# Moving every SBUF tile by a few bytes: two unused tiles in a linear-attention kernel

## The chip, the cores and the metric

The kernel runs on one core of a Trainium2 chip. The metric is the device time of one execution in microseconds (us), as the median of several runs. Engines are called by the profile's names: PE (TensorE matmul), PEld (TensorE weight load), DVE (VectorE), ACT (ScalarE), POOL (GpSimd), SP (SyncE, which here issues nearly all the transfers).

## The reference

x has 4 batches of 512 tokens and 512 features. It is layer-normalised, goes through a gated linear attention of 16 heads of 128, and is multiplied by the SiLU of a router's mixture; the input is added at the end.

```python
def _lightning_attn(x, slope_rate, w_qkv, w_gate, w_out, norm_w):
    qkv = silu(einsum('bnf,of->bno', x, w_qkv))
    q, k, v = split(qkv.reshape(b, n, h, 3 * d), 3, axis=-1)
    def step(kv, blk):
        qi, ki, vi = blk
        o_inter = einsum('bhmd,bhde->bhme', qi * q_decay, kv)
        qk = einsum('bhmd,bhnd->bhmn', qi, ki) * diag_decay
        o_intra = einsum('bhmn,bhne->bhme', qk, vi)
        kv_new = block_decay * kv + einsum('bhmd,bhme->bhde', ki * k_decay, vi)
        return (kv_new, o_inter + o_intra)
    _, out = scan(step, kv0, (qb, kb, vb))
    out = norm_w * (out * rsqrt(mean(out * out) + EPS))
    gate = sigmoid(einsum('bnf,of->bno', x, w_gate))
    return einsum('bno,fo->bnf', gate * out, w_out)

xn = layernorm(x)
s = _lightning_attn(xn, ...)
scores = softmax(xn @ router_weight.T + router_bias)
topk_w, topk_idx = top_k(scores, 8)
ffn = xn * sum(topk_w) + einsum('tk,tkh->th', topk_w, expert_bias[topk_idx])
return x + s * silu(ffn)
```

## The kernel before

**Numbers.** The large products are made of fp32 operands split into a rounded high part and the rest (split_hi on ACT, split_lo on DVE or POOL), both kept as fp32r; three passes (high by high, high by low, low by high, PASSES) stand for one full product. The attention itself and the router's logits are plain fp32, which the trace shows as two matmuls each. Each large product is made of seven products of half-size blocks (PRODUCTS, a Strassen-Winograd scheme: B11, T2, T1, B21, T3, B22, T4 on the token side, A11, S2, S1, A12, S3, S4, A22 on the weight side).

**Stages.** First x is loaded, normalised, transposed by PE against ident and split into the blocks blk_B and blk_T; beside it the v units run (v_unit, lines 565 to 584, and the first two in plain form, d_v). Their moving operand is the weights, 512 columns in one run of 2048 bytes. Then come, for each pair of batches, 8 gate units and 16 q/k units (gate_unit, qk_unit), whose weights are stationary and whose moving operand is a block, `blocks[p, xn][:, :, xi, c]`: four runs of 128 columns, 512 bytes each. All of them go through unit(), whose matmul is line 506. Between the products of one unit the attention of the head before is run: scores_qk (sa line 662, transposes kt line 665), states (ss line 685), attend (o lines 747 and 749). The last stage is the output projection over 112 steps (p, m, g), each of 12 matmuls of 256 columns (acc, line 1218): the stationary operand is yr, the moving one wr. From step 54 on to 68, after every second step, ffn (line 811) adds two matmuls of 512 columns.

**Order.** The order on each engine is the order of the code (manual_schedule). Lists of functions, `after[j]`, are run behind the j-th product of a unit.

**Where tiles lie.** SBUF is taken from two sides. A pool made by left() or without a side grows upwards from the start, one made by right() downwards from the end, like two stacks. A pool's tiles lie one behind the other, each rounded up to 32 bytes per partition. From the left: const, wk, small, xa, then xb and later o and o2, and in the first stage vw and vout. From the right: stage, vraw, vsum; then hraw, hsum, hw, att, again, xc; at the end late. const comes first on the left, and holds small tiles of which several are not multiples of 128 bytes; it adds up to 3616 bytes. Nearly all large tiles are of 1024 bytes or multiples of 512, so a side's large tiles all begin at the same place modulo 128: 32 on the left, 96 on the right.

**Operands by side.** For the v units both operands are on the left (weights in vw, blocks in xa and xb). For q/k and gate units the weights are in hw, on the right; the blocks are on the left, except that for the second pair of batches B11, T2 and T1 are loaded into xc, on the right. The attention's tiles are all in att, on the right. In the output projection, wr of m = 0 lies in o and of m = 1 and 2 in xa (left), the others in late (right); yr of every second step lies in o2 (left), hw (right, parts 2, 3, 6, 7) or late (right, every third part after part 9); a part serves two steps. ident is a const tile.

```python
    def left(stack, name, bufs=1):
        return pool(stack, name, bufs, side="left", reuse_waits="tile")

    def right(stack, name, bufs=1):
        return pool(stack, name, bufs, side="right", reuse_waits="tile")
...
        tag, bufs = ("ws", None) if pool_ is hpools["w"] else ("yr", 2 if pool_ is op2 else 1)
...
                from_ = late if nsplit > 9 and nsplit % 3 == 1 else op2
```

reuse_waits="tile" makes a tile that takes over another's space wait for the release of just the tiles it overlaps.

Of the kernel before, what the change touches and what calls it, by code (L numbers as in the profile page):

```python
# [8 lines left out]
F32 = mybir.dt.float32  # L9
# [5 lines left out]
P = 128  # L15
# [35 lines left out]
def kernel(  # L51
# [26 lines left out]
    def pool(stack, name, bufs=1, **kw):  # L78
        return stack.enter_context(tc.tile_pool(name=name, bufs=bufs, **kw))
# [5 lines left out]
    def right(stack, name, bufs=1):  # L85
        return pool(stack, name, bufs, side="right", reuse_waits="tile")

    const = pool(ctx, "const")
# [14 lines left out]
        eng.tensor_tensor(lo, src, hi.bitcast(F32), ALU.subtract)  # L103


    slopes = const.tile([P, NH], F32, tag="slopes", name="slopes")
    rb = const.tile([P, E], F32, tag="rb", name="rb")
    rw = const.tile([P, FC, E], F32, tag="rw", name="rw")
# [1118 lines left out]
    for i, (p, m, g) in enumerate(steps):  # L1227
# [15 lines left out]
        if g == 0:  # L1243
            k, first = PRODUCTS[m][2:]
            if m < 3:
                q, tag = (ps_sc, "sc") if k == 2 else (ps_mm, "mm")
# [92 lines left out]
```

## Time and profile before

| | us |
|---|---|
| median of 3 runs | 1063.43 |
| lowest, highest | 1061.49, 1067.32 |
| span of the profiled execution | 1062.1 |

The page gives the span and no separate time of that execution; the median of the runs lies 1.3 us above it. The granted TensorE clock is 0.999 on average.

| matmuls, by shape | count | busy, mean ns of one |
|---|---|---|
| acc, 128x256 | 1344 | 281 |
| u_qk, 128x512 (four groups) | 1344 | 393 to 397 |
| u_g, 128x512 (four groups) | 672 | 392 to 401 |
| u_v, 128x512 (four groups) | 588 | 389 to 396 |
| d_v, 128x512 | 96 | 391 to 402 |
| o, 128x128 | 896 | 275 |
| sa, 128x128 | 512 | 275 |
| ss, 128x128 | 384 | 274 |
| kt, 128x128 transposes | 192 | 273 |

Matmuls are pipelined, so these busy times overlap. The chain of work that ended last, asked for over a stretch of time, is merged into pieces with a count; a piece of matmuls alone, divided by its count, gives the time from one matmul's start to the next one's.

### The profile page before, as it was taken

To read this page: it belongs to the slowest core of one execution; us is meant where nothing else is said; L and a number is where in the kernel's file an instruction comes from. 1 tells how busy PE (TensorE), PEld (TensorE's weight loads), DVE (VectorE), ACT (ScalarE), POOL (GpSimd) and SP (SyncE) were. 2 spreads that over 40 slices of the span, in tenths; PEclk is the share of its full clock that TensorE was granted. 3 is DMA by queue.
4 is the path that set the end of the run, shared out by engine and by line. 5 is a ranking of instruction groups with operands and counts; after the bars stand their busy time and mean duration, and the time that the engine had idled before them with its cause. 6 is when DMAs were issued, how large, how long until landed. Compare 5 with 4: busy or idle time off the path is not lost.

```text
span 1062.1 us, 17614 instructions
## 1 busy us (share of the span) xinstructions
PE 1043.7 (98%) x6338; PEld 923.6 (87%) x6338; DVE 636.5 (60%) x1017; ACT 558.5 (53%) x969; POOL 687.7 (65%) x698
## 2 busy tenths in 40 slices
PE   8999999999999999899999999999999999999997
PEld 7888888888888878788888888888888889999997
DVE  6665543356565777675554555455555557698667
ACT  5555554655555445454554655555555546574632
POOL 4887782757788677677778687878678753124013
PEclk9999999999999999999999999999999999999999
DMA  6456747523434365564664423443233336989863
GB/s 226 167 200 245 269 146 230 161 85 115 135 116 147 130 213 186 186 216 147 238 233 125 132 86 115 154 130 114 85 106 128 105 134 215 337 303 306 283 219 102
DMA packets 128838, 185.12 MB, mean 174 GB/s; under 512 B 11104, under 2 KB 72688, under 8 KB 127856
## 3 DMA queue, kind: packets, MB, share of 16 engines
q1 hardware_dynamic: 127856, 183.56, 52.2%
q8 instruction: 50, 0.82, 0.3%
q10 hardware_dynamic: 896, 0.44, 0.1%
q14 instruction: 36, 0.29, 0.1%
HBM read 115.26 MB, written 70.80 MB: 175 GB/s over the span
## 4 chain that ended last, share of the span: by engine, by line
PE 91%; DVE 5%; DMA 2%; issue 1%; ACT 0%; SPq 0%; POOL 0%; DVEq 0%; ACTq 0%; POOLq 0%
PE u_qk L506 27%; PE u_g L506 14%; PE acc L1218 13%; PE u_v L506 13%; PE sa L662 5%; PE o L747 5%; PE o L749 4%; PE ss L685 4%; PE kt L665 2%; PE d_v L536 2%; PE lg L322 1%; DMA raw_v<-in_w_v_dram 1%; DVE wosum L736 1%; DVE yS L710 1%; DMA x<-in_x_dram 1%
## 5 line engine op out<-in xcount | busy, mean ns | idle before, releaser
L1218 PE MATMUL acc<-wr,yr 128*128 128x256 f32 x1344 | 163.4, 281 | 1.3 <-DVE a_o L890 1.3
L1218 PEld LDWEIGHTS acc<-wr,yr 128*128 128x128 f32 x1344 | 161.5, 190 | 3.2 <-DVE a_o L890 1.7
L506 PE MATMUL u_qk<-blk_T,ws_qk 128*128 128x512 f32 x576 | 148.0, 397 | 0.0
L759 POOL TENSOR_TENSOR sqs<-sqs,sq 128x512 f32<-128x512 f32 x60 | 78.2, 1303 | 91.4 <-ACT sq L758 91.4
L506 PEld LDWEIGHTS u_qk<-blk_T,ws_qk 128*128 128x128 f32 x576 | 105.7, 188 | 21.4
L103 POOL TENSOR_TENSOR ws_qk<-sum_qk,ws_qk 128x512 fp32r<-128x512 f32 x64 | 88.8, 1395 | 40.8 <-ACT ws_qk L100 40.8
L506 PE MATMUL u_qk<-blk_B,wa_qk 128*128 128x512 f32 x384 | 100.1, 396 | 0.0
L870 POOL TENSOR_TENSOR u<-u,x 128x256 f32<-128x256 f32 x28 | 32.3, 1175 | 100.3 <-DVE u L869 69.7
L103 DVE TENSOR_TENSOR yr<-yin,yr 128x1024 fp32r<-128x1024 f32 x56 | 75.6, 1355 | 35.2 <-ACT yr L100 29.8
L747 PE MATMUL o<-at,vin 128*128 128x128 f32 x512 | 88.4, 275 | 0.0
L506 PEld LDWEIGHTS u_qk<-blk_B,wa_qk 128*128 128x128 f32 x384 | 70.9, 188 | 15.0
L100 ACT CAST yr<-yin 128x1024 fp32r<-128x1024 f32 x56 | 58.4, 1046 | 44.6 <-PE acc L1218 34.4
L550 ACT ACTIVATE k<-k 128x512 f32<-128x512 f32 x64 | 40.4, 632 | 74.3 <-DVE k L497 74.3
L751 DVE SCALAR_TENSOR_TENSOR y<-o,nw,gt 128x512 f32<-128x512 f32 x64 | 48.0, 751 | 51.3 <-PE o L749 51.3
L747 PEld LDWEIGHTS o<-at,vin 128*128 128x128 f32 x512 | 74.8, 191 | 2.5
L506 PE MATMUL u_g<-blk_T,ws_g 128*128 128x512 f32 x288 | 76.5, 401 | 0.0
L671 ACT ACTIVATE kd<-kt,kdecay 128x384 f32<-128x384 f32 x64 | 37.2, 581 | 73.9 <-PE kt L665 73.9
L758 ACT ACTIVATE sq<-o 128x512 f32<-128x512 f32 x60 | 35.9, 598 | 74.3 <-POOL sqs L759 43.2
L749 PE MATMUL o<-qd,st 128*128 128x128 f32 x384 | 74.2, 275 | 0.0
L103 POOL TENSOR_TENSOR ws_g<-sum_g,ws_g 128x512 fp32r<-128x512 f32 x32 | 41.4, 1295 | 48.6 <-ACT ws_g L100 48.6
L689 DVE SCALAR_TENSOR_TENSOR st<-st,bdecay,ss 128x128 f32<-128x128 f32 x128 | 41.7, 346 | 52.1 <-ACT st L687 49.9
L673 POOL TENSOR_TENSOR qd<-q,dec 128x384 f32<-128x384 f32 x64 | 70.9, 1129 | 0.0
(199 smaller groups left out, 2434.4 us busy)
## 6 DMA issues: line engine op xcount, KB each, us to landing
yin<-y SPq DMA_DIRECT2D x56, 512.0 KB, 4.5
v<-vo_v SPq DMA_DIRECT2D x64, 256.0 KB, 2.4
raw_qk<-in_w_head_dram SPq DMA_DIRECT2D x64, 256.0 KB, 4.1
vin<-v SPq DMA_DIRECT2D x64, 256.0 KB, 3.4
y<-yS SPq DMA_DIRECT2D x64, 256.0 KB, 2.1
y<-y SPq DMA_DIRECT2D x48, 256.0 KB, 2.2
woin<-wo SPq DMA_DIRECT2D x18, 512.0 KB, 5.7
x<-in_x_dram SPq DMA_DIRECT2D x32, 256.0 KB, 4.6
```

Of the source, the lines that this page charges most:

```text
L100: nc.scalar.copy(hi, src)
L103: eng.tensor_tensor(lo, src, hi.bitcast(F32), ALU.subtract)
L506: nc.tensor.matmul(ps, lhsT, rhs, start=(first and c == 0 and n == 0), stop=(c == KC - 1 and n == len(PASSES) - 1), skip_group_check=not f ...
L662: nc.tensor.matmul(pa[:, c], k[:, c], q[:, c], start=True, stop=True)
L673: nc.gpsimd.tensor_tensor(qd[s], q[:, 1:], d[:, 1, None, :].to_broadcast([P, NT - 1, P]), ALU.mult)
L685: nc.tensor.matmul(ps[:, c], kd[s][:, c], v_of(b, h, c), start=True, stop=True)
L689: nc.vector.scalar_tensor_tensor(r[:, c], r[:, c - 1], bdecay[:, h : h + 1], ps[:, c], ALU.mult, ALU.add)
L747: nc.tensor.matmul(o, v_of(b, h, c), at[s][:, c], start=True, stop=(c == 0))
L749: nc.tensor.matmul(o, st[s][:, c - 1], qd[s][:, c - 1], start=False, stop=True)
L751: nc.vector.scalar_tensor_tensor(y, po, nw[:, h : h + 1], gts[s], ALU.mult, ALU.mult)
L759: nc.gpsimd.tensor_tensor(sq[b], sq[b], s1, ALU.add)
L1218: nc.tensor.matmul(acc[t // 2][:, t % 2], yr[:, yi, bass.ts(t, P)], wos[m, g // NQ][:, wi, g % NQ], start=(first and g == 0 and n == 0 and ...
```

## The change

Two tiles are allocated and never used: one of 24 fp32 (96 bytes per partition) as the first tile of const, on the left, and one of 8 fp32 (32 bytes) in a pool of its own, the first on the right, which stays open to the end. All tiles that come after them on their side lie 96 bytes higher or 32 bytes lower. The large tiles on the left then begin at 0 modulo 128 in place of 32, those on the right at 64 in place of 96.

```diff
+    margin = right(ctx, "margin")
+    const.tile([P, 24], F32, tag="margin", name="margin_left")
+    margin.tile([P, 8], F32, tag="margin", name="margin_right")
     slopes = const.tile([P, NH], F32, tag="slopes", name="slopes")
```

## The prediction

> **What bounds the kernel now.** I read the page from the engines down: busy shares first, then the chain of work that ended last, then that chain piece by piece in short stretches.
>
> ```profile
> PE 1043.7 (98%) x6338; PEld 923.6 (87%) x6338; DVE 636.5 (60%) x1017; ACT 558.5 (53%) x969; POOL 687.7 (65%) x698
> PE 91%; DVE 5%; DMA 2%; issue 1%; ACT 0%; SPq 0%; POOL 0%; DVEq 0%; ACTq 0%; POOLq 0%
> ```
>
> TensorE (PE) is busy nearly throughout and carries 91% of the chain, so the end moves only if a matmul takes more or less time from its start to the next one's start. The busy durations in the costliest groups (281 ns for a 256-column matmul, 397 ns for a 512-column one) overlap and can't be added. The chain can: a piece "x24" is 24 matmuls with nothing between them, so its length over its count is the true price of one. First two long pieces of the whole chain (start us, us, what):
>
> ```profile
> 99.23 88.67 PE u_v L506 x390
> ...
> 682.17 12.41 PE u_qk L506 x54
> ```
>
> 88.67/390 = 227.4 ns for the v units, whose 512 moving columns lie in one run; 12.41/54 = 229.8 ns for the q/k units, whose 512 columns are four runs of 128. Next the same chain, asked for over 945 to 1003 us, where each piece between two ffn matmuls holds two steps of the output projection, and so tells apart where their operands lie:
>
> ```profile
> 944.98 26.45 PE acc L1218 x224
> ...
> 971.90 2.73 PE acc L1218 x24
> ...
> 978.40 2.87 PE acc L1218 x24
> ...
> 981.74 2.79 PE acc L1218 x24
> ```
>
> The ffn matmuls follow steps 54, 56, 58 and so on, so the first x24 piece is steps 55 and 56, the second 59 and 60, the third 61 and 62. By the code, step 55 streams wr from the right side against weights yr on the left, and step 56 the other way round (parts 27 and 28; part 28 comes from the pool late). Steps 59 and 60 have both operands on the left. Same work, same clock (1.00 in this stretch): 2.73/24 = 113.8 ns with the operands on opposite sides, 2.87/24 = 119.6 ns on the same side. So a matmul's price here depends on where its operands lie modulo 128, and one step between the two prices is 0.14/24 = 5.8 ns. The third piece, left/left and then left/right, lies between (116.3 ns). This is what the change can move.
>
> Last, the stretch of 198 to 240 us:
>
> ```profile
> 209.88 0.89 PE sa L662 x8
> 210.77 0.33 PE kt L665 x3
> ...
> 215.08 1.34 PE ss L685 x12
> 216.42 4.14 PE u_qk L506 x18
> ```
>
> kt is the one frequent matmul whose moving tile is not at 32 modulo 64: it streams ident. The const tiles, each rounded up to 32 bytes, add up to 3616 = 28 x 128 + 32 bytes, and the left side behind them is said to lie at 32, so const starts at 0; ident stands behind 1408 = 11 x 128 bytes, also at 0. It costs 0.33/3 = 110 ns. sa and ss, also of 128 columns but with both tiles on the right, cost 0.89/8 = 111.3 and 1.34/12 = 111.7. (kt is a transpose, so part of the difference may be its own.)
>
> **The change part by part.** It adds no instruction, wait or transfer: nothing writes or reads the two tiles, and the order on every engine and queue stays. What stands in the same place is not changed either: every left tile goes up by 96 bytes and every right tile down by 32, so a left and a right tile that take each other's space come 128 bytes closer. The nearest pair that must not touch, the end of o2 and the start of att and late, is 192 bytes apart by the tile sizes and will be 64. So no new wait arises; an overlap would have cost a wait of PE on a release, of up to the 6.5 us that PE's longest wait group has now.
>
> What is left is addresses. Left minus right stays 64 modulo 128. What changes is the place within a block of 64 bytes: every large tile lay half a block off (32 and 96), and now begins a block. Priced by groups of matmuls, counts from the groups by shape:
>
> A, output projection (acc): 1344 of 256 columns, now 26.45/224 = 118.1 ns in the chain's long piece.
> B, 512 columns in one run (u_v 588, d_v 96, pu and spare 32): 716, now 227.4 ns.
> C, 512 columns in four runs (u_qk 1344, u_g 672): 2016, now 229.8 ns.
> D, two-pass fp32 (o 896, sa 512, ss 384, lg 128): 1920, now about 111.5 ns.
>
> No row shows A to C with aligned tiles, so I bound them. Below: they cost what kt shows per 128 weights loaded, 110 ns for A, and twice that for 512 columns. A saves 8.1 x 1344 = 10.9 us, B 7.4 x 716 = 5.3, C 9.8 x 2016 = 19.8, D 1.5 x 1920 = 2.9: 38.9 us. Above: the pairs on opposite sides fall to the dearer state (the slower rival below, +11 us). I take one step, 5.8 ns, off each of A, B and C: (1344 + 716 + 2016) x 5.83 ns = 23.8 us. My reason is that the prices lie on steps of that size (113.8 and 119.6), that a run starting half a block off touches one block more than it has to; if PE fetches by such blocks, which no row shows and which I suppose, every one of these matmuls pays for one. The value lies between the ends, nearer the rows of acc themselves than kt, which is another kind of matmul. D I leave at 0.
>
> The const tiles go the other way: ident from 0 to 96. The 272 transposes that stream it (kt 192, pt 64, pw 16) at 1.5 ns dearer are 0.4 us. Other engines' tiles move too; DVE, ACT and POOL hold 5% of the chain together, and I cost them at nothing because PE covers them; with the cover gone a change of 1% in all of DVE's 636.5 us would be 6.4 us. Transfers likewise:
>
> ```profile
> v<-vo_v SPq DMA_DIRECT2D x64, 256.0 KB, 2.4
> y<-yS SPq DMA_DIRECT2D x64, 256.0 KB, 2.1
> ```
>
> One leaves the left side, one the right, 256 KB each, 0.3 us apart, and only 2% of the chain is DMA. The cover is thinnest here (us, busy us of PE, PEld, DVE, ACT and POOL, clock, DMA share, GB/s):
>
> ```profile
> 895.00:945.00 50.00, 49.41 (x402) 48.06 (x401) 38.90 (x53) 32.81 (x43) 10.96 (x9) 1.00 0.91 316
> ```
>
> At 0.91 of the DMA engines, acc can run some 9% faster before the loads of y and x set the pace; one step off 118.1 is 5%, so it passes. If it did not, A's 5% in those 50 us, 2.5 us, would be lost.
>
> Two rules of the Trainium skill pull apart on this. "TensorE: Matmul & The Clock Gate", section Back-to-back issue gap, gives a warm matmul N/2.4 + 2.5 ns, 109.2 at 256 columns and 215.8 at 512; if alignment restored all of that, A, B and C would give back an estimated 12.0 + 8.3 + 28.2 = 48.5 us. "SBUF — State Buffer", section Who interferes with whom, says that PE never waits on anyone, and its read ports for weights and moving data are independent; by that addresses cost nothing and the sum is 0. The 113.8 against 119.6 ns above contradicts the second in this kernel. The same page's section on operand start alignment says it is about legality and that nothing was timed.
>
> Sum: 1062.1 - 23.8 + 0.4 = 1038.7 us of span. The median of the runs, 1063.43, lies 1.3 us above the profiled span, so 1040.0.
>
> **The rivals.** Only the distance between operands matters. It is 64 modulo 128 before and after, so all prices stay: 1063.4 us. For it: the one address effect that the profile shows is one of sides. Against it: the opposite-side price is still above kt's. The same time follows if the tiles are laid out otherwise than described.
>
> Slower: with both streams starting on a block's edge, the weights' and the moving data's reads meet at every block, and pairs on opposite sides lose their advantage. Place: u_qk and u_g with blk on the left and weights on the right, all 1008 of the first pair of batches and, since three of seven blocks then lie in xc on the right, 576 of the second, 1584 x 5.83 = 9.2 us; in acc some 720 matmuls on opposite sides at 117 on average rise to 119.6, 1.9 us. With the 0.4 us of ident: 1063.4 + 11.5 = 1074.9. It decides from 5.3 us on, about 910 such matmuls. For it: same-side pairs do pay today. Against: nothing shows why 0 and 64 should meet where 32 and 96 don't.
>
> All of the excess over kt goes: 1063.4 - 38.9 + 0.4 = 1024.9; the forecast's own lower end.
>
> **How the numbers follow.** One step or more gained (forecast and its lower end): 0.57. Distance alone, or nothing done: 0.16. Meeting streams: 0.27. A measurement here tells about 0.5%, 5.3 us, from no change. So faster 0.57, same 0.16, slower 0.27; likeliest 1040, with its own range 1025 to 1056 (a third of a step). Leaving out a little below 1025 and the worse half of the slower case, the range is 1023 to 1075.
>
> **What would show it.** Right: u_v's long piece near 221 ns a matmul in place of 227.4, 18 of u_qk in about 4.03 us in place of 4.14, acc x24 pieces all below 2.73 to 2.79 us, kt at 0.33 to 0.34 for three. Wrong: the same pieces with the same lengths (the distance rival), or acc pieces of different sides at 2.87 and u_qk x18 above 4.2 (meeting streams). A DMA or DVE share of the chain that grows past 895 us would show a gain that was not passed on. What would overturn it all is a change in DVE, ACT or POOL durations large enough to reach PE.

## The result and the profile after

The changed kernel takes 1067.34 us (median of 22 runs, 1064.11 to 1073.41), the kernel before 1065.07 us (22 runs): ratio 1.0034, 95% interval 1.0022 to 1.0047. By the ratio that is 3.6 us slower, less than 0.5% (the two medians lie 2.3 us apart). The forecast was 1040, a gain; the measured time lies in the stated range of 1023 to 1075 only because that range also took in the rivals. The profiled execution after has a span of 1067.0 us against 1062.1.

Shares of the engines and of the chain of the page after (first line: busy us, share of the span, instructions):

```profile
PE 1049.5 (98%) x6338; PEld 924.4 (87%) x6338; DVE 637.5 (60%) x1017; ACT 558.4 (52%) x969; POOL 688.0 (64%) x698
PE 90%; DVE 4%; DMA 2%; issue 1%; POOL 1%; ACT 1%; SPq 1%; DVEq 0%; POOLq 0%; ACTq 0%
```

The same instructions, the same bound. What differs is again in the pieces of the chain (start us, us, what), here those of the whole chain of the changed kernel:

```profile
119.58 69.62 PE u_v L509 x306
...
199.00 12.60 PE u_qk L509 x54
...
218.18 4.20 PE u_qk L509 x18
...
688.48 12.45 PE u_qk L509 x54
...
950.55 26.63 PE acc L1221 x228
...
1000.75 57.01 PE acc L1221 x489
```

u_v: 69.62/306 = 227.5 ns, against 227.4 before. Both its operands lie on the left, and starting at 0 modulo 128 in place of 32 gave it nothing. u_qk of the first pair of batches: 12.60/54 = 233.3 and 4.20/18 = 233.3 ns, against 4.14/18 = 230.0: dearer. Of the second pair, three of whose seven blocks lie beside the weights on the right: 12.45/54 = 230.6 against 229.8. acc: 26.63/228 = 116.8 against 118.1: cheaper. Between the ffn matmuls of the output projection, and at the transposes, in two stretches of the same chain of the changed kernel:

```profile
977.64 2.79 PE acc L1221 x24
...
984.17 2.87 PE acc L1221 x24
```
```profile
212.49 0.33 PE kt L668 x3
```

The first piece is steps 55 and 56 (2.73 us before), the second steps 59 and 60 with both operands on the left: 2.87 us, to the digit as before. kt streams ident from 96 modulo 128 in place of 0, and its 0.33 us stay.

To see where the 4.9 us between the two spans are, I took from both traces the time from each matmul's start to the next one's, put it down to the earlier of the two, and told the operands' sides apart by their pools (ns is the mean of the differences under 250 ns, us their sum with all; for u_v and d_v only where the next matmul is of the same kind):

| moving, weights | count | before ns, us | after ns, us |
|---|---|---|---|
| u_qk, u_g: left, right | 1583 | 229.5, 379.7 | 233.2, 386.0 |
| u_qk, u_g: right, right | 432 | 230.3, 102.2 | 228.9, 101.7 |
| acc: right, left | 504 | 117.8, 60.0 | 115.1, 58.0 |
| acc: left, right | 216 | 116.1, 25.1 | 117.2, 25.3 |
| acc: left, left | 360 | 120.6, 43.4 | 120.7, 43.5 |
| acc: right, right | 263 | 119.6, 33.1 | 119.6, 33.1 |
| u_v, d_v: left, left | 668 | 227.3, 154.4 | 227.4, 156.7 |
| fp32, two-pass: right, right | 1791 | 108.6, 194.5 | 108.7, 194.7 |

One row carries the loss: u_qk and u_g with the block on the left and the weights on the right, 1583 x 3.7 ns = 5.9 us. acc with wr right and yr left gives back 504 x 2.7 = 1.4 us. acc with both operands on one side keeps its price; u_qk and u_g with both on the right get 1.4 ns cheaper, 0.6 us. By the ns alone the sum is +4.4 us, inside the interval of the ratio (2.3 to 5.0 us). The 2.3 us more of u_v and d_v are nearly all in two places where PE waited for DVE, some 0.9 us at 19.7 us (a wait for w_A_v) and 1.1 us at 118.2 us (for e_v); the mean price of a u_v matmul is the same. The profiled execution of e1 below has the second wait and not the first, that of e4 the first and not the second, so neither belongs to the change alone; what makes them was not looked for.

### The profile page after: what moved, and what is told of

It reads as the page before. It is cut to its first block, busy times and chain, and to the rows that moved or that the text cites. A ratio compares the mean times of both kernels' runs of the same rounds, so it can differ in the third digit from the quotient of the medians.

```text
span 1067.0 us, 17614 instructions
## 1 busy us (share of the span) xinstructions
PE 1049.5 (98%) x6338; PEld 924.4 (87%) x6338; DVE 637.5 (60%) x1017; ACT 558.4 (52%) x969; POOL 688.0 (64%) x698
## 4 chain that ended last, share of the span: by engine, by line
PE 90%; DVE 4%; DMA 2%; issue 1%; POOL 1%; ACT 1%; SPq 1%; DVEq 0%; POOLq 0%; ACTq 0%
PE u_qk L509 27%; PE acc L1221 14%; PE u_g L509 14%; PE u_v L509 12%; PE sa L665 5%; PE o L750 5%; PE o L752 4%; PE ss L688 4%; PE kt L668 2%; PE d_v L539 1%; PE lg L325 1%; DMA raw_v<-in_w_v_dram 1%; DVE wosum L739 1%; DVE yS L713 1%; POOL w_S_v L103 1%
```

## The experiments

Two theories were left. D: a matmul's price goes by the distance between its moving operand and its weights, with a period of 256 bytes or more. (A distance is given modulo 256; both theories are about where a tile starts in its partition.) Before the change the right side began 192 bytes behind the left modulo 256; the change moved the sides towards each other by 128 and made it 64, which modulo 128 is the same. P: the place within 64 or 128 bytes counts. The change altered both at once; the first two experiments alter one each.

**e1: the distance alone.** One unused tile of 128 bytes on the left; every tile keeps its place modulo 128, the distance is 64.

```diff
+    const.tile([P, 32], F32, tag="margin", name="margin_left")
     slopes = const.tile([P, NH], F32, tag="slopes", name="slopes")
```

> One unused tile of 128 bytes on the left alone. Every tile keeps its place modulo 128 (left 32, right 96), but the right side now begins 64 bytes behind the left modulo 256, as after the change, where it was 192. Theory D (only the distance between a matmul's two operands counts, modulo 256 or more): the time of the changed kernel, ratio to before 1.002 to 1.005; 18 matmuls of u_qk with blk left and weights right 4.20 us in place of 4.14; acc with wr right and yr left 114 ns in place of 118. Rival P (the place modulo 64 or 128 counts): as before, ratio 1.000 +- 0.001, 4.14 us.

Measured: ratio 1.0039 (1.0022 to 1.0056). The chain of e1 from 198 us on:

```profile
210.36 0.33 PE kt L666 x3
...
216.05 4.20 PE u_qk L507 x18
```

The price of the changed kernel without its alignment: u_qk and u_g left/right (the moving operand on the left, the weights on the right) 233.2 ns, acc right/left 115.3.

**e2: the place alone.** by_row goes from the left to the first place on the right, so that both sides sink by 32 bytes: 0 and 64 modulo 128 as after the change, and the distance of before.

```diff
-    by_row = const.tile([P, 2], F32, tag="rest_of", name="rest_of")
+    margin = right(ctx, "margin")
+    by_row = margin.tile([P, 2], F32, tag="rest_of", name="rest_of")
```

> No unused tile; the tile by_row (32 bytes with its rounding) moves from the left to the first place on the right. Both sides lie 32 bytes lower: left at 0 and right at 64 modulo 128 as after the change, their distance as before (192 modulo 256). Theory D: the time of before, ratio 1.000 +- 0.001, 18 u_qk matmuls 4.14 us, acc right/left 118 ns. Rival P: the time of the changed kernel, ratio 1.002 to 1.005, 4.20 us, 114 ns.

Measured: ratio 1.0000 (0.9984 to 1.0015), and in its chain

```profile
216.66 4.14 PE u_qk L507 x18
```

as before. The table's prices are those of before as well (229.6; acc 117.8 and 116.0). So the place within 64 or 128 bytes moves nothing that can be seen here, and the distance moves all that the change moved. P falls. The pairs whose two operands both lie on the left are a further control: in the twelve profiled kernels the left side stands at eight different places modulo 256, and u_v costs 227.3 to 227.7 ns in all of them, acc left/left 120.5 to 120.7 in all but v1, which alone moves yr against wr.

**e3 and e4: two more distances.** Unused tiles of 64 and 192 bytes on the left: distances 128 and 0. (Here and for s1 to s3 the comment behind a line names its run.)

```diff
+    const.tile([P, 16], F32, tag="margin", name="margin_left")    # e3
+    const.tile([P, 48], F32, tag="margin", name="margin_left")    # e4
```

> One unused tile of 64 bytes on the left: both sides at 96 modulo 128, the right 128 bytes behind the left modulo 256. Theory D with a period of 128: pairs on opposite sides now cost what pairs on one side cost: acc 120 ns throughout (some 720 matmuls by 3 ns, +2 us), u_qk and u_g between the 228 and 231 ns of their right/right matmuls, so +-3 us: ratio 0.999 to 1.005. With a period of 256: a price of its own for opposite pairs, not that of one side. Rival P: left tiles move by 64 within a block of 128, so pairs of one side on the left change from 120 and 227 ns too; under D these stay.

> One unused tile of 192 bytes on the left: both sides at 96 modulo 128, and at the same place modulo 256 (distance 0; one side against itself has distance 0 as well). Theory D: opposite pairs cost what one side costs, acc 120 ns throughout (+2 us), u_qk and u_g 228 to 231 ns: ratio 0.999 to 1.005. If e3 and e4 have the same prices the period is 128, else 256 or more. Rival P: as e3, since both sides lie at the same places modulo 128.

Measured: e3 1.0047 (1.0031 to 1.0063), e4 0.9989 (0.9975 to 1.0003). Chain of e3, at 198 to 240 us, and of e4 at the same place:

```profile
216.74 4.18 PE u_qk L507 x18
```
```profile
216.28 4.10 PE u_qk L507 x18
```

Both sides start at 96 modulo 128 in both kernels, and yet u_qk and u_g left/right cost 232.4 ns in one and 227.8 in the other: the period is not 128. At distance 0, acc costs 120.3 to 120.6 on opposite sides, as on one side (119.8 and 120.6); u_qk and u_g cost 227.8, below every price of theirs until then. I had expected 228 to 231 there.

**s1 to s4: the odd distances**, one run each for their prices. Unused tiles of 32, 96 and 160 bytes on the left, and for the fourth one tile less there:

```diff
+    const.tile([P, 8], F32, tag="margin", name="margin_left")     # s1
+    const.tile([P, 24], F32, tag="margin", name="margin_left")    # s2
+    const.tile([P, 40], F32, tag="margin", name="margin_left")    # s3
```
```diff
-    ones = const.tile([P, 1], F32, tag="ones", name="ones")
-    mhalf = const.tile([P, NT], F32, tag="mhalf", name="mhalf")
+    halves_ones = const.tile([P, NT + 1], F32, tag="mhalf", name="mhalf")
+    mhalf, ones = halves_ones[:, 0:NT], halves_ones[:, NT:]
```

> One unused tile of 32 bytes on the left: the right begins 160 bytes behind the left modulo 256. Measured so far, one u_qk or u_g matmul with blk left and weights right costs 229.6 ns at 192, 232.5 at 128, 233.2 at 64, 227.8 at 0. Theory D, smooth in the distance: between its neighbours, about 231 ns, acc on opposite sides 117 to 119.5; one side against itself stays at 120 (acc) and 227.4 (u_v). Rival (blocks of 64 bytes count, so that 32 is a straddle): a price outside the two neighbours.

> One unused tile of 96 bytes on the left and none on the right: left at 0 modulo 128 as in the change, right at 96 as before; distance 96. Theory D, smooth: 232.5 to 233.2 ns for u_qk and u_g, acc right/left between 115.4 and 119.4, left/right 117.3 to 119.4. Rival (blocks): outside these.

> One unused tile of 160 bytes on the left: distance 32. Theory D, smooth: u_qk and u_g between 227.8 and 233.2 ns, about 230.5; acc right/left 115.4 to 120.6, left/right 117.3 to 120.3. Rival (blocks): outside these.

> The const tiles mhalf and ones share one tile, which takes 32 bytes off the left: distance 224. Theory D, smooth: u_qk and u_g between 227.8 and 229.6 ns, acc right/left 117.8 to 120.6, left/right 116.4 to 120.3; u_v and acc on one side stay at 227.4 and 120. Rival (blocks): outside these.

The runs took 1072.4, 1071.8, 1068.9 and 1069.3 us beside one of 1063.4 of the kernel before; a single run each, so only their prices are used. D in its smooth form was wrong: u_qk and u_g lie outside their neighbours at 32, 96 and 160 and at the upper edge at 224, and acc lies outside at 96. The rival's forecast, a price outside, thus came true for u_qk and u_g, whose odd distances cost 233.2 to 234.0 ns, and for acc at 96, but not for acc at 32, 160 and 224. Why the prices run as they do over the distance is open. Put together, though, the eight distances give each price twice. With wr on the right and yr on the left, moving minus weights is the distance; with wr on the left it is 256 minus the distance, from another kernel:

| moving minus weights, modulo 256 | acc, wr right, ns | acc, wr left, ns | u_qk and u_g, left/right, ns |
|---|---|---|---|
| 0 | 120.6 (e4) | 120.3 (e4) | 227.8 (e4) |
| 32 | 117.5 (s3) | 117.6 (s4) | 233.3 (s4) |
| 64 | 115.1 (after), 115.3 (e1) | 116.1 (before) | 229.5 (before) |
| 96 | 120.1 (s2) | 120.4 (s1) | 233.4 (s1) |
| 128 | 119.5 (e3) | 119.4 (e3) | 232.4 (e3) |
| 160 | 117.8 (s1) | 118.6 (s2) | 234.0 (s2) |
| 192 | 117.8 (before) | 117.2 (after) | 233.2 (after, e1) |
| 224 | 118.8 (s4) | 119.0 (s3) | 233.2 (s3) |

The two columns of acc agree within 1.0 ns in every row, though one streams from the right and the other from the left and, but for 0 and 128, each row comes from different kernels. In this table side and place drop out; what is left is moving minus weights modulo 256. It also has a sign: 64 and 192 are not alike, clearly for u_qk and u_g (229.5 against 233.2). The change swapped just these two. A price of acc is a mean, though, over stretches at two levels, near 113 and near 118 ns, and both occur at 64 and at 192: at 64, 57% (before) and 71% (after) of the differences are 115 ns or less, at 192 only 15% and 34%.

**d0 and v1: the distance within one side, and a faster kernel.** By the table u_qk and u_g cost least at 0 and acc at 64. d0 takes 64 bytes off the left (distance 0, this time 256 modulo 512):

```diff
-    ones = const.tile([P, 1], F32, tag="ones", name="ones")
-    mhalf = const.tile([P, NT], F32, tag="mhalf", name="mhalf")
+    few = const.tile([P, NT + 3], F32, tag="mhalf", name="mhalf")
+    mhalf, ones = few[:, 0:NT], few[:, NT : NT + 1]
...
-    by_row = const.tile([P, 2], F32, tag="rest_of", name="rest_of")
+    by_row = few[:, NT + 1 :]
```

v1 adds two pads that put yr 64 bytes before wr:

```diff
                 op2 = left(o_stack, "o2", 2)
+                op2.tile([P, 48], F32, tag="pad", name="pad_left", bufs=1)
...
         if i == 16:
+            late.tile([P, 16], F32, tag="pad", name="pad_right", bufs=1)
             load_eb(late)
```

> mhalf, ones and by_row share one const tile, which takes 64 bytes off the left: distance 0 modulo 256 again, but 256 modulo 512, where e4 had 0 modulo 512. Theory D with a period of 256: the prices of e4, u_qk and u_g at 227.8 ns with blk left and weights right, acc 120 to 120.6 on opposite sides, ratio 0.998 to 1.000. With a period of 512 or more: other prices, 229 ns and more. Theory P has no account of e4's 227.8.

> As d0_left_minus_64, and two pads inside pools (192 bytes at the start of o2, 64 bytes behind yr in late) put yr 64 bytes before wr modulo 256 in 104 of the 112 steps, whichever side they lie on. Theory D: the price goes by the distance whatever the side, so acc on one side falls from 120.5 too; at 115.2 to 116.4 ns for some 1247 matmuls (the best prices of the runs so far) it saves 5 to 7 us against d0, ratio to before 0.990 to 0.994. Rival (what counts is being on two sides): acc pairs of one side stay at 120, ratio 0.997 or above.

Measured: d0 0.9988 (0.9978 to 0.9999), v1 0.9935 (0.9915 to 0.9954). The chain of d0, pieces of the output projection from its whole chain and from 930 to 1010 us:

```profile
942.24 27.34 PE acc L1218 x228
...
993.33 58.67 PE acc L1218 x489
```
```profile
970.04 2.86 PE acc L1218 x24
...
973.37 2.86 PE acc L1218 x24
...
976.69 2.86 PE acc L1218 x24
```

With all distances 0, every piece is 2.86 us, 119.2 ns a matmul, whatever the sides; x489 gives 120.0. v1, its chain from 935 us on and its whole chain:

```profile
976.24 2.83 PE acc L1219 x24
...
982.84 2.72 PE acc L1219 x24
...
986.02 2.83 PE acc L1219 x24
```
```profile
97.68 88.67 PE u_v L506 x390
...
989.32 57.60 PE acc L1219 x489
```

57.60/489 = 117.8, with left/left pairs down from 120.5 to 118.0 and right/right from 119.8 to 116.5 in the table's measure: a pair on one side gets cheaper when its operands move apart within that side. But the table's price for 64 did not carry over whole: at that distance acc costs 116.5 to 118.0 ns in v1, also with wr right and yr left (117.1, where the changed kernel has 115.1). So the distance is not all that sets the price of acc. u_v, untouched by the pads, is at 227.4. v1 beats both kernels, by 0.65% the one before and, by the two ratios, by about 1% the changed one. The gain of d0 is in u_qk and u_g (227.8 ns) less the loss in acc; v1 takes that loss back. Of the 5 to 7 us that I expected of the pads against d0, the means of acc (120.2 to 117.6 over 1343 matmuls) explain 3.6; the medians differ by 4.9; where the rest comes from was not looked for. v1's ratio met its forecast, then, though its price of acc did not. d0 and e4 have the same prices at 0 and at 256 modulo 512, which is what makes the period 256; it was tried at this one distance.

## Why the prediction was wrong

**What bounds the kernel**: right. But for the two short waits above, all that moved, moved in the chain's matmuls.

**No new wait, transfers and other engines at nothing**: right as far as the runs show. e2, which moves all large tiles by 32 bytes, has the ratio 1.0000, and e1, with the distance alone, the ratio of the change; the matmuls' prices, +4.4 us, leave nothing of the measured 3.6 us for other engines to explain.

**"Every large tile lay half a block off (32 and 96), and now begins a block", and one step of 5.8 ns off each of A, B and C**: this is the step that failed. B, u_v, went from 227.4 to 227.5 ns. A on one side stayed (2.87 us in 24); on opposite sides it fell by 2.7 ns one way round and rose by 1.1 the other. C rose by 3.7 ns in 1583 matmuls, those with the block on the left. The term put at -23.8 us measured some +4.2 (A -1.1, B 0, C +5.3). e2 shows that the place within a block is worth nothing by itself. The block was supposed, not read: the two prices of acc, 113.8 and 119.6 ns, told of the distance between operands, and I took the size of that effect as the price of another. The size was misread too: 113.8 ns is one piece of 24, and over all matmuls of acc on opposite sides the kernel before has 117.8 and 116.1 ns, so the gap to one side (119.6 and 120.6) is some 2 to 4.5 ns and not 5.8.

**A reading that led there**: "the moving tile is not at 32 modulo 64" was offered for kt's 110 ns. kt at 96 modulo 128 costs the same 0.33 us for three, and from start to start 109.1 to 109.3 ns in all twelve kernels, wherever ident lies and at whatever distance from k. Its price tells nothing of alignment, and the bounds of A to C built on it had no ground. Nor did the 0.4 us for ident.

**The rival "only the distance between operands matters"** had the mechanism and the wrong period: "It is 64 modulo 128 before and after, so all prices stay". Modulo 256 it went from 192 to 64. The trace before held a hint: acc pairs with distance 64 modulo 128 both ways, at 116.1 ns with wr left and 117.8 with wr right. I averaged over the difference. Had I read it as a price for 64 and another for 192, the swap follows: acc right/left falls to the price of left/right and back, (504 x -1.7 + 216 x 1.7) = -0.5 us; and for the 1584 left/right matmuls of u_qk and u_g, which before stood at 64, the cheaper of the two in acc, a loss, though of a size that nothing before the change told.

**The slower rival** named the place that lost, 1584 matmuls of u_qk and u_g, and a wrong mechanism: streams that meet on a block's edge would have met in e2 too. Its 5.8 ns measured 3.7, and its loss of 1.9 us in acc was a gain of 1.1 us. That it had the right sign and place is luck.

**The two rules of the Trainium skill.** "SBUF — State Buffer", Who interferes with whom, says that PE never waits on anyone and calls its two read ports independent. By the prediction addresses then cost nothing. d0 and v1, 120.0 and 117.8 ns a matmul in the same 489, and e1 show that they do cost: the price goes with the difference between the starts of the moving operand and the weights. Whether the two reads meet at SBUF or elsewhere no run shows, so the runs contradict the conclusion drawn from the rule and not the rule itself. The N/2.4 + 2.5 ns of "TensorE: Matmul & The Clock Gate", Back-to-back issue gap, 215.8 ns at 512 columns, is the page's figure for an isolated matmul; for a stream of weight loads and matmuls the page says that it over-counts at large N. Here no distance brought the mean at 512 columns below 227 ns.

## What to carry to other kernels

Before moving tiles for alignment, tell matmuls apart by where their moving operand lies against their weights, as one difference modulo 256 and with its sign, and read a price for each from all pieces of the chain with a count, not from one. A shift that keeps a difference modulo 128 can still change it modulo 256, and a kernel's tiles of one kind can be moved by a pad of 64 bytes without touching its code's order. Shift both operands alike when you want to test place against distance: that one run (e2) would have settled the supposition on which the forecast stood.

## What was unexpected in the hardware

The price of one fp32r matmul depends on moving minus weights modulo 256 bytes: 115 to 121 ns at 256 columns in one run, 228 to 234 ns at 512 columns in four runs, at a mean clock of 0.995 and above. The best distance differs between the two shapes (64 and 0). For 512 columns in one run (u_v) and for plain fp32 with both tiles on the right only the distance 0 was tried; kt, an fp32 transpose, keeps its 109 ns at every distance it had. At one distance and one shape there are two levels: at 64 the matmuls of one step of acc mostly cost either 113 to 114 or 117 to 118 ns each and stay there, as v1's pieces of 2.72 and 2.83 us show, and at 192 the same two occur (in the kernel before, step 30 at 113.3 ns and step 47 at 117.8). The mean for a distance is thus largely the share of its steps at each level; what picks the level was not tried. Why the price has this form is open. PEld is busy 87% of the span beside 98% of PE, so weight loads run while matmuls stream, and that the two disturb each other is a guess that no run tests. And the 432 right/right matmuls of u_qk and u_g, whose own distance never changed, cost 230.3 ns before, 228.9 after and 227.9 in e4: they stand between matmuls whose distance did change, but that their neighbours carry over is not shown.
